# Relative attention with paired corner terms, a reordered unit, a reordered start, and reordered experts

## Chip, core and metric

The kernel runs on one core of one Trainium2 chip. The metric is the device time of one execution in microseconds (us); lower is better. All tensors are float32. Every input comes from device memory (DRAM) and the output goes back there.

## The reference, cut

Four layers follow one another on 16 sequences of 256 tokens with 128 features, each with a layer norm over the sum with its input: an attention with relative positions, six local-attention layers, a causal attention, and a mixture of experts. The change touches the first and the last.

```python
def _L0_attn_ref(x, Wq, Wk, Wv, Eq, Ek, Ev):        # 16 heads of 8
    rel = jnp.clip(r[:, None] - r[None, :], -64, 64) + 64
    q, k, v = (proj(Wq), proj(Wk), proj(Wv))
    a_q, a_k, a_v = Eq[rel], Ek[rel], Ev[rel]
    content = jnp.einsum('bhld,bhmd->bhlm', q, k)
    rel_k = jnp.einsum('bhld,lmd->bhlm', q, a_k)
    rel_q = jnp.einsum('bhmd,lmd->bhlm', k, a_q)
    pos_pos = jnp.einsum('lmd,lmd->lm', a_q, a_k)
    attn = jax.nn.softmax((content + rel_k + rel_q + pos_pos) * scale, axis=-1)
    return jnp.einsum('bhlm,bhmd->bhld', attn, v) + jnp.einsum('bhlm,lmd->bhld', attn, a_v)
```

The experts: each token takes the two best of eight experts by a softmax of gate scores (`gate_w`); an expert is `gelu(x @ w1 + b1) @ w2 + b2` with 64 hidden units.

## The kernel before

**Engines and order.** PE (TensorE) multiplies and transposes into PSUM, DVE (VectorE), ACT (ScalarE) and POOL (GpSimd) do the rest, SP sends DMAs. PSUM is given out as two tiles of 128x1024 (`big`) and four of 128x512 (`small`). Within a layer the program is a list of small steps written out by hand (`TURNS`, one row for each of eight slots; the number ahead of a step says how many batches, or units, it lags or, if negative, runs ahead). `in_order(first)` then fixes, for PE, ACT, DVE and POOL, the program's order of all instructions from index `first` on; SP is left to the scheduler. In relative attention `first` is taken after the tables' set-up.

**Relative attention.** A batch is eight units: 128 query rows (`lc`) by four heads. `weights` (a unit's logits, L501) puts into one `big` tile, for four heads, 256 key columns in two halves: `o = 0`, the 128 keys of the query's own half, and `o = 1`, the others. Two kinds of matmul add up there: transposes of stored terms (`rk3`, and `rkc3` for `o = 1`, L513) and products of 32 rows (`q` or `qe` with `ks`, L525). In the other half, relative distances beyond 64 all use one clipped row, so that only a corner of 64 keys by 64 queries (per `lc`) differs from it; `rkc3` holds a block of 128x128 for each head with that corner in it and zeros elsewhere, and the constant part sits in `qe` and `ks`. DVE (L535) adds the third term `rq3` and takes the minimum; `exponentials` (ACT, L551) and `turn_weights` (PE L570, copies by ACT or DVE) follow one and two units later, then `positions` and `values`.

The terms are made a batch ahead: `turn` and `project` (q, k; L317, L326), `rearranged` (POOL copies into the one tile `r_perm`, four stores to DRAM, L388, and four loads into `spots`, L393), `diagonal` (POOL mask, L405), `rq_half`, `rk_half` (PE L419, 32-row matmuls), `rq_corners`, `rk_corners` (PE L444, 32x64 matmuls), with copies by ACT (L458, L467) and adds by DVE (L478, L488). Slot 4 holds, in order for PE: `join`, `weights`, `rq_half`, `turn_weights`; slot 5: `rq_corners`, `weights`, `turn_weights`; slot 6: `project_v`, `weights`, `rq_half`, `positions`, `rk_half`, `rq_corners`, `turn_weights`; slot 7: `weights`, `rk_corners`, `turn_weights`.

Set-up, from L757: memsets of `rq3` and `rkc3`; loads; the tables `tq`, `tk` from `Eq`, `Ek` (`toeplitz`, L793); the product row `frow`, stored as `fx`; then windows of `evx` and `fx` loaded as `win` tiles and turned over by a matmul with `anti` (L878) into `tv`, `tvc`, `pp`, `ppc`. `run(at)` for `at` from -8 to -1 makes the terms of batch 0; the loads of x for batches 2 to 15 stand at `at == 0`.

**Experts.** Eight groups `g` of 512 tokens. `turn` and `score(h)` for four groups at a time, `choose(h)` (DVE, and one POOL step, L1812 to L1829) picks the experts; `first(g)` is the first matmul with Gelu (PE L1840, ACT L1847), `turn_gates` transposes the gates (L1854), `weigh` spreads them (PE L1865) and multiplies them onto the Gelus (DVE L1867, `e_hT`), `second` is the second matmul (L1876, L1883) with the residual (`e_y`) and moments on DVE, reciprocal root on POOL (L1897, L146), and `finish` normalises on ACT (L1907) and stores.

## Time and profile before

| | us |
|---|---|
| median of three runs (4126.4 to 4129.33) | 4128.36 |
| the profiled execution | 4126.21 |
| its span, first to last instruction | 4124.3 |
| PE busy | 4012.5 |
| DVE busy | 3285.5 |
| ACT busy | 3305.0 |
| POOL busy | 2783.4 |
| first transposes of logits (L513) | at 57.4 |
| last of them | at 716.8 |
| first instructions of the experts' loads | at 4000.5 |
| granted PE clock, mean | 0.991 |

An engine's busy time counts an instruction from its start to its end; matmuls are pipelined, so that several overlap and a busy PE need not be at its peak. "Idle <- X" is time in which an engine stood and what ended it; "issue" is a wait for nothing that the profile shows. The chain of waits is followed back from the last instruction, at each step to what released it. Lines of it read: start, length, what. Lines of the timeline read: start, length, engine, line, operation, output <- inputs, shape, how many merged.

### The profile page before, as it was taken

Reading aid. Unit: us, or ns where it says so; the run is one execution under the profiler, and the core shown is the slowest. Engines: PE = TensorE matmul, PEld = TensorE weight load, DVE = VectorE, ACT = ScalarE, POOL = GpSimd, SP = SyncE. Lnnn points to the kernel's source line nnn. Section 1 sums busy time; section 2 is a strip of 40 time slices with the busy share of each in tenths; the row PEclk is TensorE's granted clock in tenths of the full one; section 3 lists DMA queues with packets and bytes.
Section 4 is the critical chain, followed back from the end, with each engine's and each line's share of the span. In section 5 each row is a group of like instructions: output and inputs, shape, how many; then the busy total and the mean of one; then the engine's idle time right before and its main releaser. Section 6 shows DMA issues by size and latency. Waiting matters only on the chain.

```text
span 4124.3 us, 141653 instructions
## 1 busy us (share of the span) xinstructions
PE 4012.5 (97%) x57932; PEld 2937.4 (71%) x57932; DVE 3285.5 (80%) x6379; ACT 3305.0 (80%) x11434; POOL 2783.4 (67%) x3334
## 2 busy tenths in 40 slices
PE   7999999899999999999999999999999999999998
PEld 5888888567677677667767776776777767656665
DVE  4666666788888888888888888888888888779974
ACT  3777766688888888888888888888888888879973
POOL 3333332788888888888888888888888888722221
PEclk8999999999999999999999999999999999999999
DMA  2101012100000000000000000000000000000000
GB/s 62 40 29 38 31 36 64 26 16 19 21 24 19 15 20 20 25 21 20 20 25 16 19 19 20 25 21 14 21 15 24 15 16 14 9 3 2 2 8 21
DMA packets 181813, 90.03 MB, mean 22 GB/s; under 512 B 142493, under 2 KB 173220, under 8 KB 181164
## 3 DMA queue, kind: packets, MB, share of 16 engines
q1 hardware_dynamic: 181164, 80.97, 7.4%
q8 instruction: 457, 7.49, 0.8%
q14 instruction: 192, 1.57, 0.1%
HBM read 38.49 MB, written 6.31 MB: 11 GB/s over the span
## 4 chain that ended last, share of the span: by engine, by line
PE 86%; POOL 6%; ACT 3%; issue 2%; DVE 1%; DMA 1%; SPq 0%; POOLq 0%; DVEq 0%; ACTq 0%
PE small L1250 16%; PE big L1100 12%; PE small L1157 8%; PE big L1225 7%; PE big L1172 5%; PE small L1347 3%; PE small L1331 3%; PE small L1315 3%; PE small L570 3%; PE big L525 3%; POOL a_u L1139 3%; PE small L1592 3%; PE big L1548 3%; PE big L513 3%; PE small L1225 2%
## 5 line engine op out<-in xcount | busy, mean ns | idle before, releaser
L1193 ACT ACTIVATE a_pr<-a_pr,a_nb 128x64 f32<-128x64 f32 x3072 | 1024.0, 338 | 5.7 <-DVE a_nb L1186 5.7
L1121 POOL TENSOR_TENSOR a_u<-a_u,a_r 128x1024 f32<-128x1024 f32 x384 | 901.3, 2371 | 25.9 <-DVE a_r L1116 21.2
L1139 POOL TENSOR_TENSOR a_u<-a_u,a_y 128x1024 f32<-128x1024 f32 x384 | 722.9, 1904 | 15.0
L1250 PE MATMUL small<-a_vo,a_g 128*128 128x128 f32 x6144 | 718.1, 275 | 1.6 <-DVE c_st L1465 1.6
L1250 PEld LDWEIGHTS small<-a_vo,a_g 128*128 128x128 f32 x6144 | 701.6, 192 | 2.6 <-ACT a_g L1243 2.5
L1111 ACT ACTIVATE a_sq<-big 128x1024 f32<-128x1024 f32 x384 | 391.4, 1021 | 260.2 <-PE big L1100 259.5
L1193 ACT ACTIVATION_READ_ACCUMULATOR a_pr<-a_pr,a_nb 128x1 f32 x3072 | 587.9, 191 | 0.0
L1157 PEld LDWEIGHTS small<-ident,a_u 128*128 128x128 f32 x3072 | 349.7, 141 | 142.8 <-POOL a_u L1139 91.0
L1128 DVE TENSOR_REDUCE a_ss<-a_sq 128x16 f32<-128x1024 f32 x384 | 445.6, 1200 | 0.0
L1157 PE MATMUL small<-ident,a_u 128*128 128x128 f32 x3072 | 402.3, 274 | 25.3 <-POOL a_u L1139 23.4
L1100 PE MATMUL big<-w_k,a_xs 128*128 128x512 f32 x768 | 382.0, 620 | 5.1 <-DVE a_r L1116 2.1
L1205 POOL TENSOR_TENSOR a_pr<-a_pr,a_rd 128x1024 f32<-128x1024 f32 x192 | 366.1, 1907 | 13.0 <-DVE a_rd L1204 13.0
L1100 PE MATMUL big<-w_q,a_xs 128*128 128x512 f32 x768 | 361.4, 593 | 0.0
L1172 PEld LDWEIGHTS big<-a_kT,a_qT 64*32 64x32 f32 x24576 | 261.4, 105 | 124.7 <-issue 74.8
L1180 DVE TENSOR_TENSOR a_pr<-big,w_band 128x1024 f32<-128x1024 f32 x192 | 234.6, 1222 | 109.0 <-PE big L1172 109.0
L535 DVE CUSTOM_DVE_ANT_0 r_lg<-big,r_rq 128x256 f32<-128x256 f32 x512 | 186.7, 421 | 152.7 <-PE big L525 126.4
L1112 DVE TENSOR_TENSOR a_u<-big,a_tak 128x1024 f32<-128x1024 f32 x192 | 235.1, 1224 | 83.9 <-ACT a_sq L1111 83.9
L1172 PE MATMUL big<-a_kT,a_qT 64*32 64x64 f32 x24576 | 293.1, 225 | 6.4 <-POOL a_kT L1150 3.5
L1233 ACT COPY a_g<-big 128x1024 f32<-128x1024 f32 x192 | 193.7, 1009 | 107.3 <-PE small L1225 106.8
L1100 PEld LDWEIGHTS big<-w_q,a_xs 128*128 128x128 f32 x768 | 142.6, 190 | 162.6 <-issue 127.4
L551 ACT ACTIVATE r_lg<-r_lg,r_nb 128x256 f32<-128x256 f32 x512 | 254.4, 508 | 2.8 <-DVE r_nb L535 2.8
L1574 ACT ACTIVATE c_lg<-c_lg,c_nb 128x256 f32<-128x256 f32 x512 | 255.6, 513 | 0.1
(290 smaller groups left out, 9316.9 us busy)
## 6 DMA issues: line engine op xcount, KB each, us to landing
a_xm<-a_xt SPq DMA_DIRECT2D x96, 96.0 KB
r_dk<-r_rowsk SPq DMA_DIRECT2D x64, 128.0 KB
r_dq<-r_rowsq SPq DMA_DIRECT2D x64, 128.0 KB
f_xt<-xa SPq DMA_DIRECT2D x96, 64.0 KB
f_xt<-xa SPq DMA_DIRECT2D x96, 63.5 KB
a_xt<-xa SPq DMA_DIRECT2D x80, 64.0 KB
a_xt<-xa SPq DMA_DIRECT2D x80, 63.5 KB
w_k<-in_L_ffn_Wqkv_dram SPq DMA_DIRECT2D x6, 512.0 KB
```

Source lines behind the costliest of these rows:

```text
L1100: T.matmul(ps[:, c * 512 : (c + 1) * 512], lhsT=xs_of[i, b][:, t, 0:P], rhs=weights[i]["qk"[j]][:, c * 512 : (c + 1) * 512], start=True, s ...
L1111: A.activation(sq, ps3, AF.Square)
L1121: G.tensor_add(u, u, r)
L1128: V.tensor_reduce(ss[:, j], st[m]["sq", j], AX.X, ALU.add)
L1139: G.tensor_mul(u, u, bcast(y[:, j].unsqueeze(2), (P, H, DH)))
L1157: T.transpose(ps[:, k, :], u[:, o : o + P], ident)
L1172: T.matmul(ps[q0 : q0 + WIN, e, c, :], lhsT=qT[DH * e : DH * (e + 1), c, q0 : q0 + WIN], rhs=kT[DH * e : DH * (e + 1), c, t * P + q0 : t * ...
L1193: A.activation(s_["pr"][:, h], s_["pr"][:, h], AF.Exp, bias=s_["nb"][:, h : h + 1], accum_out=s_["den"][:, h : h + 1],)
L1205: G.tensor_mul(s_["pr"], s_["pr"], bcast(rd.unsqueeze(2), (P, H, DH)))
L1225: T.matmul(ps[win], lhsT=x[r, t, :], rhs=pT[r, :, o, :], start=(o == 0), stop=(o == 1),)
L1250: T.matmul(ps[:, 0:D], lhsT=st[m]["g"][:, h, :], rhs=weights[i]["vo"][:, h // 2, h % 2, :], start=(h == 0), stop=(h == H - 1),)
L1574: A.activation(lg[:, j], lg[:, j], AF.Exp, bias=nb[:, j : j + 1], scale=-1.0, accum_out=st[b, lc]["den"][:, h : h + 1],)
```

## The change

It has four parts.

1. Corner terms: `rkc3` holds two heads in one block of 128x128, the even head's corner on partitions 0 to 63 and the odd head's on 64 to 127; `rk_corners` writes each with two adds, one for each parity. One transpose, whose output is 64 columns of each of two heads, takes the place of two.
2. In `weights` the products come first, then the corner transposes, then the four of `rk3`.
3. The start: `in_order` covers SP as well and begins ahead of the set-up; batch 0's `turn`, `project` and `rearranged` (split into `there` and `back`) stand in the midst of the set-up, and the windows are loaded and turned at other places; `qe` is made in `shift`; memsets of `rq3` cover its second half alone, and some stand later.
4. Experts: `choose(h)` follows `score(h)`; `first` runs three groups ahead; `weigh(g + 1)` stands before `second(g)`; the last group's moments, normalisation (on DVE) and store are done in two halves, the first of them inside the loop of its matmuls.

```diff
-    def in_order(first):
+    def in_order(first, engines=ENGINES):
...
-            rkc3[k] = pool.tile([P, H, P], F32, name=f"r_rkc{k}")
+            rkc3[k] = pool.tile([P, H // 2, P], F32, name=f"r_rkc{k}")
...
+            if b:
+                shift(b)
+
+        def shift(b):
+            q, qe = st[b]["q"], fea.tile([P, S], F32, name="r_qe")
...
         def rearranged(b, n):
+            there(b, n)
+            back(b, n)
...
             for k in range(2):
                 rows, l0 = slice(MAXD * k, MAXD * k + MAXD), MAXD * (1 - k) + 32 * phase
-                V.tensor_add(
-                    of(rkc3, b, k)[rows, :, l0 : l0 + 32].rearrange(
-                        "p h (x g i) -> p x g h i", x=2, i=4
-                    ),
-                    ps[rows],
-                    bcast(pc[rows], (MAXD, 2, 4, H, 4)),
-                )
+                for e in range(2):
+                    V.tensor_add(
+                        of(rkc3, b, k)[MAXD * e : MAXD * e + MAXD, :, l0 : l0 + 32].rearrange(
+                            "p h (x g i) -> p x g h i", x=2, i=4
+                        ),
+                        ps[rows].rearrange("p x g (h e) i -> p e x g h i", e=2)[:, e],
+                        bcast(pc[rows], (MAXD, 2, 4, H // 2, 4)),
+                    )
...
-            for o in range(2):
-                for j, h in enumerate(hs):
-                    T.matmul(
-                        ps[:, j // 2, j % 2, o],
-                        lhsT=of(rkc3 if o else rk3, b, lc)[:, h, :],
-                        rhs=ident,
-                        is_transpose=True,
-                        start=(o == 0 and j % 2 == 0),
-                        stop=False,
-                    )
             for o in range(2):
                 for k in range(2):
...
                         lhsT=s_["qe" if o else "q"][r, L],
                         rhs=s_["ks", lc][r, x : x + 2, o, :],
-                        start=False,
-                        stop=(o == 1),
+                        start=(o == 0),
+                        stop=False,
                     )
+            for k in range(2):
+                T.matmul(
+                    ps[:, k, :, 1, MAXD * lc : MAXD * lc + MAXD],
+                    lhsT=of(rkc3, b, lc)[:, hs[2 * k] // 2, :],
...
+            for j, h in enumerate(hs):
+                T.matmul(
+                    ps[:, j // 2, j % 2, 0],
+                    lhsT=of(rk3, b, lc)[:, h, :],
...
-        G.memset(rq3[0], 0.0)
-        for k in range(2):
-            V.memset(rkc3[k], 0.0)
...
+            first = len(nc.cur_bb.bb.instructions)
             load_x(0)
+            for n in "qk":
+                nc.sync.dma_start(w[n], I[f"L0_attn_W{n}"])
...
+            turn(0)
+            project(0)
+            there(0, "k")
...
+            winv = windows("v", evx, HD, P * HD, whole)
+            back(0, "k")
+            there(0, "q")
+            nc.sync.dma_start(fx, frow)
+            winvc = windows("vc", evx, HD, MAXD * HD, corner)
+            back(0, "q")
+            for k in range(2):
+                rows, u = slice(MAXD * k, MAXD * k + MAXD), (NEXT - 1) * k
+                nc.sync.dma_start(fe[rows], fx[0:1, u : u + 1].rearrange("a b -> (a b)").partition_broadcast(MAXD))
+            winp = windows("p", fx, 1, P, whole)
+            winpc = windows("pc", fx, 1, MAXD, corner)
...
+            nc.sync.dma_start(w["v"], I["L0_attn_Wv"])
+            load_x(1)
+            nc.sync.dma_start(pick, I["pick"].rearrange("p (g m) -> p g m", g=4))
+            shift(0)
+            for k in range(2):
+                G.memset(rq3[k][:, :, 1], 0.0)
+            turned(tv.rearrange("p s d -> p (s d)"), winv, HD, P * HD, None)
+            for k in range(2):
+                V.memset(rkc3[k], 0.0)
+            for at in range(-NU, -NU + 6):
+                run(at)
+            turned(pp, winp, 1, P, None)
+            turned(ppc, winpc, 1, MAXD, fe)
+            turned(tvc.rearrange("p s d -> p (s d)"), winvc, HD, MAXD * HD, ee)
...
+        for at in range(-NU + 6, N + NU):
+            if at == -NU + 6:
+                G.memset(spread, 0.0)
+            if at == -1:
+                G.memset(rq3[2][:, :, 1], 0.0)
+                V.memset(rkc3[2], 0.0)
             if at == 0:
                 for b in range(2, NB):
                     load_x(b)
             run(at)
-        env.in_order(first)
+        env.in_order(first, (*ENGINES, mybir.EngineType.SP))
...
-        glp = ctx.enter_context(tc.tile_pool(name="e_glp", bufs=NH + 1))
+        glp = ctx.enter_context(tc.tile_pool(name="e_glp", bufs=4))
...
-            if g % 2:
+            if g in (1, 3):
                 V.tensor_copy(xT, ps)
...
+                if g == NG - 1 and k % NT == NT - 1:
+                    close(g, k // NT)
+            if g < NG - 1:
+                measure(g)
...
+        def close(g, j):
+            y = two.tile([P, NT, D], F32, name="e_yh")
+            added(y, g, j)
+            mv, rs = moments(y)
+            for t in range(NT):
+                V.tensor_scalar(
+                    y[:, t], y[:, t], mv[:, t, 0:1], rs[:, t : t + 1], ALU.subtract, ALU.mult
+                )
+            store(g, j, y)
...
             score(h)
-        choose(0)
-        for g in range(NH):
-            first(g)
+            choose(h)
+        first(0)
+        first(1)
         turn_gates(0)
         weigh(0)
-        choose(1)
+        first(2)
+        turn_gates(1)
         for g in range(NG):
-            if g + 1 < NG:
-                turn_gates(g + 1)
-            if g + NH < NG:
-                first(g + NH)
-            second(g)
+            if g + 3 < NG:
+                first(g + 3)
             if g + 1 < NG:
                 weigh(g + 1)
+            second(g)
+            if g + 2 < NG:
+                turn_gates(g + 2)
             if g:
                 finish(g - 1)
-        finish(NG - 1)
         env.in_order(begin)
```

## The prediction

> **What bounds the kernel now.** I read the page's slices first: TensorE (PE) is busy in nine tenths or more of every slice but the first and the last, and its granted clock is full except there.

> ```profile
> PE   7999999899999999999999999999999999999998
> PEclk8999999999999999999999999999999999999999
> ```

> The middle (local_layers and causal_attention, lines 900 to 1727) is not edited, so three stretches matter. First, the chain of waits of the first 58 us, before the first unit of logits (its transposes start at 57.45).

> ```profile
> 8.49 7.08 PE small L793 x16
> 31.25 5.50 DMA r_rowsq<-r_perm
> 38.30 5.43 DMA r_dq<-r_rowsq
> 43.74 2.06 DMA xb<-in_L_attn_x_dram
> 50.39 7.67 issue
> ```

> Read: batch 0's q goes through DRAM and lands only at 43.7; before that PE made the tables (L793) ahead of batch 0's projection (L326 at 18.44), and POOL's mask of q (L405) started at 45.8. It is a latency chain, PE mostly idle. Second, the timeline of PE in a steady unit.

> ```profile
> 316.12 1.09 PE L570 MATMUL small<-ident,r_lg 128*128 128x128 f32 x8
> 317.05 0.60 PE L513 MATMUL big<-ident,r_rk 128*128 128x128 f32 x4
> 317.49 0.60 PE L513 MATMUL big<-ident,r_rkc 128*128 128x128 f32 x4
> 318.02 0.70 PE L525 MATMUL big<-r_ks,r_q 32*128 32x256 f32 x4
> 318.55 0.60 PE L525 MATMUL big<-r_ks,r_qe 32*128 32x256 f32 x4
> 319.08 1.10 PE L586 MATMUL small<-r_pT,r_tv 128*32 128x64 f32 x64
> ```

> Read: starts follow each other without a wait, so PE sets the end here; four transposes take 0.44 (317.05 to 317.49), 0.109 each, though one is listed at 0.27. A batch takes 42.0 (L326 at 97.87 and, five batches on, at 308.07); ACT is busy 72% and DVE 65% between 160 and 400. Third, the chain at the end.

> ```profile
> 4104.90 0.75 DVE e_y L1886 x2
> 4107.32 1.12 DVE e_hT L1867
> 4108.48 2.36 PE small L1876 x8
> 4115.13 0.76 DVE e_y L1886 x2
> 4118.02 1.05 POOL e_rs L146
> 4119.70 0.49 ACT e_o L1907
> ```

> Read: a round of experts from group 4 on takes 10.2 and is no PE round: `second` ends, DVE adds and takes moments, only then multiplies `e_hT`, and PE stands for 2.0 to 2.6 (2.62 before 4108.48).

> **Head of attention.** Removed: the tables ahead of batch 0 and 10.5 us of POOL memsets (3 x 3.5; now three halves of `rq3`). By the issue rows (0.34 to 1.54 each), SP has sent the loads listed ahead of `there(0, "k")` by about 9.0. x goes out at 0.72; its landing is not shown: rows of other loads give 2.2 (e_gw) to 3.9 (r_extq), so 2.9 to 4.6, I take 4. Then transposes 0.7, copy 0.4, projections 2.1, two copies 0.7: k at 8 instead of 21.2. POOL's rearrangement 0.7, to 8.9. SP: four stores 2.5, to 11.5; `winv` 0.6, to 12.1; four loads 2.8 to 3.5, to 15.3; landing 5.4 after the last issue (38.30 row), and 1 to 2 more behind winv's 512 KB (a slot of the DMA row moved 291 GB/s): 22, against 36.8. POOL may rearrange q when the stores have read `r_perm` (28.35 to 29.89, 1.5): 13.8. SP: stores 2.5, `fx` 0.3, `winvc` 1.1, loads 2.8: 22.2; q's blocks land at 27.7 to 29, against 43.7.
> The new order adds waits. On SP everything now stands behind the four loads of q, so `fe`, `winp`, `winpc` (2.9) are out at 25.1 and land 3.2 after issue (26.02 to 29.20), up to 28.5 behind q. PE's `turned(pp)` waits for them; behind it in PE's order stand rq_half 1 and rk_half 1. With 1.5 for the turns and 1.6 for rq_half 1 the first rk_half runs at 31.6 instead of 47.74: **-16.1**. From there to the first logits is DVE's drain, 9.7 before and after (8.2 of L478 and L488). The x loads of batches 2 to 15 (14 x 0.6 on SP) fall between about 29 and 38, ahead of batch 1's k stores near 44, so they cost nothing; without that cover, up to 8. Bounds: -9 (each landing 3 later, twice, and one more), -18. Batch 1's k still needs its own trip (PE idles 70.2 to 72.8 already), so what four units save there, 0.9, is lost: head **-15.2**.

> **Units.** 128 units lose two of eight term transposes: 256 x 0.109 = **-27.9**. Products ahead of transposes move the changes of array shape. From rows: entering 32-row products from 128 rows costs 0.09 + 0.12 (317.82 to 318.02, then 0.53 for 4 x 0.107), leaving them 0.1 (0.53 again): 0.3 to 0.35 a pair. With rq_half directly after products (slots 4 and 6) nothing was paid; now transposes stand between: +0.35 each. Slot 7 (rk_corners after products) +0.18. Slot 5 (rq_corners before products) saves one entry and pays one shape: -0.07. Per batch 0.81, **+13.0** over 16. Bounds 0 and 17 (slot 5 saving nothing, slot 7 a whole pair).

> [...] The rows show 0.1 to 0.2 a side.

> `rk_corners` goes from two adds of 64x512 (1.39 a pair) to four of 64x256, a form with moved partitions that the trace lacks: nearest row L478 128x256, 0.35 apart, so 1.4; bounds 1.4 and 2.8 a phase. DVE's wait for PE at 311.19 (2.06) hides it; with no cover it is 1.4 x 32 = 45. Terms are needed later in the unit, which gives them 1.0 more slack. POOL, ACT and SP of a steady batch stay. Units: **-14.9**.

> **Experts.** `choose(0)` runs 6 earlier (from 4010.8, 9.0 long), but ACT's exponential of `score(1)` now waits for DVE behind it, to 4020.6; queued behind that on ACT are the table load 1.28 and the Gelus of `first(0)`, and PE waits for their PSUM. Carrying it on (Gelu from 4022.2, `first(1)` to 4026.4, gates, weigh to 4028.9, `first(2)` and `first(3)` 3.44 each, weigh 1.07, gates 0.6) `second(0)` starts at 4037.5, was 4038.5: -1.0, bounds +3 and -4. Then `e_hT` of the next group is made while `second` (4.56) runs, so rounds are PE's: 4 x 9.56 (as 4065 to 4074 shows), 2 x 6.06 (4.56 + 1.07 + 0.43), 2 x 4.56 = 59.5, was 76.5 (4038.5 to 4115.0): -17.0, and -9 if half the waits stay. Moments of the last group by halves: from PE's end DVE 1.25, POOL 1.1, DVE 0.7, store 3.0 (4121.35 to the end), 6.1 for 9.3: -3.2. Four `glp` buffers suffice: the fourth group ahead is taken after its weigh. Experts: **-21.2**.

> **Sum.** -15.2 - 14.9 - 21.2 = -51.3. The profiled execution took 4126.21, span 4124.3 and 1.9 around it; it lies 2.15 under the runs' median of 4128.36, so 4074.9 becomes **4077**.

> **The rivals.** (a) The head does not come forward: SP in strict order stops behind one landing, windows after q, and the gain is 3 (for: 13 us of the old chain are DMA trips; against: they wait on POOL and PE work that has gone): 4089. (b) Experts stay a latency chain, the Gelus late, gain 8: 4090. (c) Changes of shape are hidden under weight loads, which overlap (PEld idles only 0.17 to 0.33): 4064. (d) It does not do what it says: PE's 100% is modelled, and another engine sets the batch; units give nothing: 4092. Against: the starts above leave no room, and DVE and ACT have a third free. (e) Slower: a transposed term accumulates onto a product just written and waits for its write. Price: at most the 0.374 of a product, for each of four heads, 1.5 a unit, 191 in all: 4268. It decides from 0.40 a unit (51.3/128). Against it: L1876 adds four terms into one block at 0.11 apart.

> **How the numbers follow.** Forecast 0.46; (a) 0.14; (b) 0.14; (c) 0.13; (d) 0.05; (e) 0.06; 0.02 for no change. A change under 0.2% (8 us) can't be told from none. Faster: 0.92, same 0.02, slower 0.06. The forecast's own range is 4064 to 4090 (bounds of its terms added as independent ones); with (a) to (c) and (d) at their middle, 4055 to 4098.

> **What would show it.** First transposes of a unit at 40 to 43; a plain unit of 2.74 instead of 2.96; L326 41.1 apart; six L513-type transposes a unit; gaps of about 0.2 before L419 in slots 4 and 6; no PE idle before L1876 from group 4 on; PE's last matmul near 6 before the end. Wrong would make it: a batch at or above 42.0, DVE without idle time, or PE waiting for `winp` beyond 35.

## The result, and the profile after

The changed kernel takes **4094.12 us**, median of four runs (4091.59 to 4097.64), beside 4127.82 for the kernel before in the same series (4126.4 to 4129.33): a ratio of 0.9919, 95% interval 0.9902 to 0.9936. So it is faster by 34 us, where 51 were forecast. The profiled execution of it took 4097.64 (span 4095.9), the slowest of the four; a second profile of the same kernel, taken later beside the experiments, took 4093.36 (span 4091.6), and both are used below.

The page's slices of the changed kernel, TensorE's busy tenths and its granted clock:

```profile
PE   8999999899999999999999999999999999989999
PEclk9999999899999999999999999999999999999999
```

The first slice is fuller than before. The clock has a dent in slice 8 (717 to 819 us; 0.90 there, 0.95 in the kernel before), which begins where the attention has just handed over to the local layers. A digit 9 stands for 0.9 or more: slice 7, with 0.93, hides the stretch at half speed that is read below.

To see where the time went, I cut the span at four instructions of TensorE that both kernels have: the projections of batches 2 and 15 (L326), the first matmul of the local layers (L1100, now L1135), and the first gate scores of the experts (L1793, now L1828). Each cell is the length of a stretch in us; the forecast gives each batch of units its -0.93 (14.9 by 16).

| stretch | before | after | again | change | forecast |
|---|---|---|---|---|---|
| start to projection of batch 2 | 97.71 | 86.14 | 85.28 | -11.6, -12.4 | -16.1 |
| 13 batches, to that of batch 15 | 546.64 | 539.36 | 539.50 | -7.3, -7.1 | -12.1 |
| to the first local matmul | 87.90 | 96.36 | 93.04 | **+8.5, +5.1** | -1.9 |
| local and causal layers | 3270.60 | 3269.46 | 3269.19 | -1.1, -1.4 | 0 |
| experts | 121.45 | 104.58 | 104.59 | -16.9, -16.9 | -21.2 |
| span | 4124.3 | 4095.9 | 4091.6 | -28.4, -32.7 | -51.3 |

All three parts gained, each less than forecast, and a stretch that I had not costed gave 5 to 8 us back.

**Head.** TensorE's timeline, changed kernel (start, busy time, engine, line, operation, tiles; in brackets idle time before it and what ended it):

```profile
31.82 0.77 PE L873 MATMUL small<-r_winp,r_anti 128*128 128x128 f32 x2 [3.44 <-DMA r_winp<-r_fx]
32.38 0.53 PE L873 MATMUL small<-r_winpc,r_anti 128*128 128x64 f32 x2
32.70 2.02 PE L873 MATMUL small<-r_winvc,r_anti 128*128 128x512 f32 x2
34.65 0.58 PE L431 MATMUL big<-r_dk,r_tq 32*128 32x128 f32 x2
...
35.02 0.42 PE L431 MATMUL big<-r_dk,r_tq 32*128 32x128 f32 x2
...
35.23 0.42 PE L431 MATMUL big<-r_dk,r_tq 32*128 32x128 f32 x2
...
36.52 0.42 PE L431 MATMUL big<-r_dq,r_tk 32*128 32x128 f32 x2
```

The turned windows wait for `r_winp`, and rq_half 1 (34.65), which needs none of them, stands behind them; rk_half, the first reader of `r_dq`, begins at 36.52.

**Units.** The same view of a steady unit:

```profile
340.71 0.70 PE L530 MATMUL big<-r_ks,r_q 32*128 32x256 f32 x4
341.24 0.60 PE L530 MATMUL big<-r_ks,r_qe 32*128 32x256 f32 x4
341.77 0.44 PE L538 MATMUL big<-ident,r_rkc 128*128 128x128 f32 x2
342.04 0.60 PE L547 MATMUL big<-ident,r_rk 128*128 128x128 f32 x4
342.48 1.04 PE L593 MATMUL small<-ident,r_lg 128*128 128x128 f32 x8
343.45 0.48 PE L530 MATMUL big<-r_ks,r_q 32*128 32x256 f32 x2
```

Six transposes of terms instead of eight, and 340.71 to 343.45 is 2.74, as forecast for a plain unit. But the batch is 41.49 (539.36 by 13), not 41.1. The wait that makes most of the difference is seen at the change of batch, first on VectorE, then on TensorE:

```profile
328.87 0.08 DVE L558 DVE_READ_ACCUMULATOR2_ANT r_nb<- 128x1 f32 x1
328.87 1.73 DVE L503 TENSOR_TENSOR r_rkc<-big,r_ppc 64x256 f32<-64x256 f32 x4
```

```profile
330.65 0.69 PE L456 MATMUL big<-r_dq,r_tkc 32*64 32x64 f32 x32 [0.27 <-DVE r_rkc L503]
```

The four adds of slot 7 (1.73; two took 1.39 before) stand behind the four reductions of a unit's logits (L558), and the next corner matmuls need the PSUM that the adds still read. Before, TensorE had no such wait.

**Hand-over.** VectorE, TensorE, ScalarE and TensorE again, changed kernel:

```profile
686.66 0.29 DVE L965 TENSOR_SCALAR w_rot<-w_rot 128x256 f32<-128x256 f32 x1 [7.31 <-DMA w_qs<-in_L_ffn_q_scale_dram]
```

```profile
687.24 1.97 PE L593 MATMUL small<-ident,r_lg 128*128 128x128 f32 x8 [2.80 <-DVE r_y L664]
```

```profile
721.43 0.37 ACT L1075 COPY a_xs<-small 128x256 f32<-128x256 f32 x1 [4.83 <-DVE xb L692]
```

```profile
721.86 3.78 PE L1135 MATMUL big<-w_k,a_xs 128*128 128x512 f32 x4 [4.23 <-ACT a_xs L1075]
```

The same two places of TensorE in the kernel before:

```profile
706.73 1.09 PE L570 MATMUL small<-ident,r_lg 128*128 128x128 f32 x8 [2.06 <-DVE r_y L641]
...
732.25 1.98 PE L1100 MATMUL big<-w_k,a_xs 128*128 128x512 f32 x4 [0.58 <-ACT a_xs L1040]
```

Two stalls. A multiply of the *next* layer's rotary table (`load_rotary`) stands among VectorE's last attention instructions and waits 7.31 us for a load; TensorE stops for 2.80 and then runs eight transposes in 1.97, as against 1.04 in a steady unit: its granted clock is 0.50 there. Then ScalarE's first copy of the local layers waits for the attention's last normalise, and TensorE stops for 4.23, where it stopped 0.58 before. TensorE by stretches of 2 us (columns: length, busy time and count of PE, PEld, DVE, ACT, POOL, granted clock, DMA share, GB/s):

```profile
684.00:686.00 2.00, 0.43 (x4) 0.20 (x2) 0.00 (x0) 1.09 (x6) 0.00 (x0) 1.00 0.66 163
686.00:688.00 2.00, 0.76 (x4) 0.77 (x5) 1.34 (x7) 0.00 (x0) 0.34 (x1) 0.59 0.76 205
688.00:690.00 2.00, 2.00 (x10) 1.58 (x10) 1.91 (x9) 0.59 (x1) 0.97 (x4) 0.50 0.09 21
...
698.00:700.00 2.00, 2.00 (x56) 1.67 (x58) 1.12 (x7) 0.96 (x4) 0.00 (x0) 0.50 0.08 17
700.00:702.00 2.00, 2.00 (x62) 1.82 (x55) 0.90 (x3) 0.00 (x0) 0.00 (x0) 1.00 0.26 51
```

The clock column falls to 0.50 during the stall (0.59 is the mean of its slice) and stays there to 700: 13.6 us at half speed.

**Experts.** TensorE's timeline of two rounds and of the last one:

```profile
4070.75 1.14 PE L1900 MATMUL big<-e_wT,e_esel 32*128 32x512 f32 x8 [0.73 <-ACT e_wT L1891]
...
4077.72 1.14 PE L1900 MATMUL big<-e_wT,e_esel 32*128 32x512 f32 x8 [0.73 <-ACT e_wT L1891]
...
4086.42 1.16 PE L1912 MATMUL small<-e_w,e_hT 128*128 128x128 f32 x8 [0.66 <-DVE e_yh L1938]
```

Of the waits of 2.0 to 2.6 before `second`, nothing is left, but two of 0.73 for the copy of turned gates have appeared (a round of 6.97, where 6.06 was forecast), and one for VectorE's read of the first half.

### The profile page after: what moved, and what is told of

It is laid out like the page before. It is cut to its first block, busy times and chain, and to the rows that moved or that the text cites. A ratio compares the mean times of both kernels' runs of the same rounds, so it can differ in the third digit from the quotient of the medians.

```text
span 4095.9 us, 141197 instructions
## 1 busy us (share of the span) xinstructions
PE 4006.0 (98%) x57676; PEld 2910.4 (71%) x57676; DVE 3299.3 (81%) x6445; ACT 3298.4 (81%) x11432; POOL 2774.8 (68%) x3334
## 4 chain that ended last, share of the span: by engine, by line
PE 72%; POOL 6%; ACT 3%; issue 2%; DVE 1%; POOLq 0%; DMA 0%; DVEq 0%; ACTq 0%; SPq 0%
PE small L1285 16%; PE big L1135 13%; PE small L1192 8%; PE big L1260 7%; PE big L1207 5%; PE small L1382 3%; PE small L1366 3%; PE small L1350 3%; PE small L1627 3%; POOL a_u L1174 3%; PE big L1583 3%; PE small L1260 2%; PE small L1643 1%; ACT a_g L1268 1%; POOL a_u L1156 1%
## 5 line engine op out<-in xcount | busy, mean ns | idle before, releaser
L1192 PE MATMUL small<-ident,a_u 128*128 128x128 f32 x3072 | 403.0, 274 | 24.5 <-POOL a_u L1174 21.1
L1135 PE MATMUL big<-w_k,a_xs 128*128 128x512 f32 x768 | 382.9, 621 | 4.6 <-ACT a_xs L1075 4.2
L1135 PE MATMUL big<-w_q,a_xs 128*128 128x512 f32 x768 | 362.0, 594 | 0.6 <-DVE a_r L1151 0.6
L558 DVE CUSTOM_DVE_ANT_0 r_lg<-big,r_rq 128x256 f32<-128x256 f32 x512 | 186.7, 421 | 132.3 <-PE big L547 81.2
L1135 PEld LDWEIGHTS big<-w_q,a_xs 128*128 128x128 f32 x768 | 142.8, 191 | 163.6 <-issue 126.8
```

Of the source, the lines that this page charges most:

```text
L1135: T.matmul(ps[:, c * 512 : (c + 1) * 512], lhsT=xs_of[i, b][:, t, 0:P], rhs=weights[i]["qk"[j]][:, c * 512 : (c + 1) * 512], start=True, s ...
L1192: T.transpose(ps[:, k, :], u[:, o : o + P], ident)
```

## The experiments

Twelve runs, in four groups; within a group all kernels and the kernel before ran on the same chip. Unless said otherwise an edit is made to the changed kernel. The intervals of single edits overlap (each is some 0.15% wide on either side), so the trace of each run carries the verdict on its place, and the time only that on the whole.

### The two stalls of the hand-over

**The multiply, taken away.** The scale goes into the constant that the table is loaded from:

```diff
     rot = np.stack([cos * scale, sin * scale, cos * inv, sin * inv])
+    rot[0:2] *= f(QK_SCALE)
...
-            V.tensor_scalar_mul(rot[:, 0:2], rot[:, 0:2], QK_SCALE)
```

> The changed kernel with the rotary table's first two planes multiplied by 8 in the constant, so that VectorE's multiply of w_rot is gone. Theory of the hand-over: that multiply, put by the scheduler among VectorE's last attention instructions, waits 7.31 us for a load (w_qs), stops TensorE for 2.80 us at 687.24 and the clock falls for some 13 us after it; without it 4 to 6 us are saved (about 4089), TensorE's idle time at 687 is gone and the granted clock between 680 and 700 is full. Rival: the load's next reader waits in its place, and the time stays within 1 us of the changed kernel's 4094.

Measured: 4089.35, ratio 0.9900 (0.9886 to 0.9913). TensorE has no idle time there, and its clock in the same stretch of 20 us is full. First the changed kernel, then this run:

```profile
680.00:700.00 20.00, 17.20 (x151) 13.68 (x144) 6.98 (x35) 9.00 (x30) 1.66 (x4) 0.66 0.25 59
```

```profile
680.00:700.00 20.00, 19.20 (x280) 15.72 (x278) 11.72 (x50) 14.26 (x48) 2.16 (x6) 1.00 0.26 64
```

From the projection of batch 15 to the last product of the attention it is 67.85 us, as against 76.84 in the first profile of the changed kernel and 73.36 in the second. The load's later readers did not stop TensorE. The theory holds; the rival falls.

**The memory places, put back.** `rkc3` is half as large after the change, so every later tile lies elsewhere. The edit allocates it whole again:

```diff
-            rkc3[k] = pool.tile([P, H // 2, P], F32, name=f"r_rkc{k}")
+            rkc3[k] = pool.tile([P, H, P], F32, name=f"r_rkc{k}")[:, 0 : H // 2]
```

> The changed kernel with r_rkc allocated as large as before (16 heads, half of it unused), so that every later tile lies where it lay before. Theory of the overlay: the halved r_rkc moved a_xs and the tables onto memory that the last normalise of the attention still reads; with the old places ScalarE's wait of 4.83 us ahead of the first a_xs copy and TensorE's 4.23 us ahead of line 1135 are gone, and the time falls by 4 to 6 us (about 4089). Rival: the wait comes of the order of the instructions alone, which stays: within 1 us of 4094.

Measured: 4090.22, ratio 0.9902 (0.9888 to 0.9915). ScalarE's copy, in this run:

```profile
714.57 0.37 ACT L1075 COPY a_xs<-small 128x256 f32<-128x256 f32 x1 [1.18 <-DVE r_rd L666]
```

The wait for the last normalise is gone, and TensorE's idle time behind it is 0.58, as before. The wait of 4.2 stood in every kernel tried with the small tile, and in none with the large one (this run, the unpaired one below, and the three that add this edit to others). So the places make it. In this run's profile the way from the last product to the first local matmul is hardly shorter for it (19.06, with 19.51 and 19.68 in the changed kernel's two), because the clock stood at 0.50 from 706.0 to 712.8; where it stayed full there, in the run of both edits, it is 15.87. On which of the tiles that the normalise reads `a_xs` lies, these runs do not show.

**Both.**

> The two edits of the hand-over together: the rotary planes scaled in the constant and r_rkc allocated as large as before. Theory (two separate stalls): the gains add, 8 to 12 us below the changed kernel in the same runs, with neither the idle time at 687 nor that of 4.2 us ahead of line 1135. Rival (one shared cause, the clock that halves for some 6.5 us after any gathering of idle time): the second edit gives nothing on top of the first, 4 to 6 us in all.

> The changed kernel itself once more, beside the three variants of it that follow, as the time to compare them with; about 0.992 of the kernel before. If the half-speed stretch of the clock at 686 to 700 belongs to the kernel, it is there again; if it belongs to that one execution, it is not.

Measured: 4083.68, ratio 0.9889 (0.9874 to 0.9904); the changed kernel itself in the same series 4092.75, ratio 0.9911 (0.9895 to 0.9928). So 9.1 us between the medians, in the range of two separate stalls; neither is left in the trace.

The half-speed stretch was in the second profile of the changed kernel too, but 6.8 us long instead of 13.6. It does not belong to the kernel, though. The run of the tail's edit (below) has the changed kernel's instructions up to the experts and the same stall, and a full clock behind it:

```profile
687.45 1.09 PE L593 MATMUL small<-ident,r_lg 128*128 128x128 f32 x8 [2.18 <-DVE r_y L664]
```

```profile
680.00:700.00 20.00, 17.82 (x281) 14.73 (x273) 10.13 (x46) 10.48 (x34) 1.67 (x4) 1.00 0.25 62
```

Seven profiles have the changed start and order, and the multiply. In four the clock fell at the stall, for 13.6, 6.8, 6.8 and 3.4 us (stalls of 2.80, 2.15, 2.19 and 3.12); in three it stayed full for 19 to 20 us more (stalls of 2.35, 1.94 and 2.18). From the projection of batch 15 to the last product TensorE's same instructions took 67.85 without the stall, 70.25 with it at full clock, 73.36 with 6.8 us at half speed and 76.84 with 13.6. So the stall itself costs 2.4, and the clock's share, 0 to 6.6 here, depends on the execution.

**How much of the first stall is old?** The kernel before had it as well (2.06 us idle at 706.73). The same edit to the constant was made to the kernel before:

> The kernel before, with the rotary planes scaled in the constant and nothing of the change. Here TensorE's idle time at 706.7 was 2.06 us and the clock stayed full. If the stall belonged to the old kernel as well, 1.5 to 2.5 us are saved and no more; if the change made it, nothing is saved; if what costs is the clock that falls after such a stall, it depends on the execution whether 2 or 6 are saved.

> The kernel before, a second profile. Its first profile showed 2.06 us of idle TensorE at 706.7 and a full clock after it; without the multiply (the run above) the time fell by about 8 us, 4 to 12 by the interval, where the trace shows 2.2. If the clock falls in some executions of the old kernel too, this one may show a stretch at half speed behind that wait, 3 to 7 us longer from the last product to the first local layer; if it is full again, the rest of those 8 us lies elsewhere and stays open.

Measured: 4123.31 beside 4131.4, ratio 0.9981 (0.9972 to 0.9990). The trace shows 2.2 of it: from the projection of batch 15 to the last product 70.52, as against 72.68. The second profile of the kernel before (4124.45) has the stall again, 2.29 long, and a full clock after it, so a falling clock does not account for the other 6; where they come from stays open. So the stall is old. The half clock behind it was seen only with the change, in four profiles of seven and in none of two before; that is too few to say that the change makes it, and why the clock falls in one execution and not in another isn't settled.

### The units: order, pairs and adds

**Products first, but no pairs.** Corner terms as before: two adds, eight transposes.

```diff
-            for k in range(2):
-                T.matmul(
-                    ps[:, k, :, 1, MAXD * lc : MAXD * lc + MAXD],
-                    lhsT=of(rkc3, b, lc)[:, hs[2 * k] // 2, :],
...
+            for o in (1, 0):
+                for j, h in enumerate(hs):
+                    T.matmul(
+                        ps[:, j // 2, j % 2, o],
+                        lhsT=of(rkc3 if o else rk3, b, lc)[:, h, :],
```

> The changed kernel with the corner terms as before (one head to a block, two adds on VectorE a phase, eight transposes a unit) but the products still ahead of the transposes. The forecast's prices: 256 transposes are worth 27.9 us, and the two further adds have since shown 0.27 us of TensorE's time a batch, 4.3 us; so 23.6 us slower than the changed kernel, about 4117, period of a batch 42.84 (42.03 before and 0.81 for the changes of array shape). Rival: putting the products first costs nothing, the period is 42.03, as before, and the time about 4103.

Measured: 4115.09, ratio 0.9961 (0.9948 to 0.9975); a batch 42.95, and no wait at line 456. The rival's 4103 is 12 away. The order alone costs 0.90 a batch (42.95 less 42.05, the same thirteen batches before). The traces show where: TensorE goes from 32-row to 128-row matmuls or back 25 times a batch where it went 21 times, and the distances from start to start across these changes sum to 5.82 instead of 4.53; starts with no such change between them take 0.39 less.

**The corner adds ahead of the reductions.**

```diff
-                (0, weights),
                 (-1, rk_corners, 1),
+                (0, weights),
                 (1, normalise, 0),
```

> The changed kernel with rk_corners 1 of slot 7 ahead of the unit's logits in place of behind them. Theory: the wait of TensorE at line 456 for r_rkc (0.27 us in each batch) is the price of the four adds standing behind the four reductions; with the adds ahead of them it is gone, 4.3 us in 16 batches, about 4090. Rival: the adds then hold the reductions back, the logits' space in PSUM is freed later by as much, and the time is the same or some us longer.

Measured: 4087.96, ratio 0.9898 (0.9885 to 0.9912); a batch 41.14. VectorE in this run:

```profile
325.06 1.72 DVE L503 TENSOR_TENSOR r_rkc<-big,r_ppc 64x256 f32<-64x256 f32 x4
326.81 0.42 DVE L558 CUSTOM_DVE_ANT_0 r_lg<-big,r_rq 128x256 f32<-128x256 f32 x1
...
328.45 1.28 DVE L490 TENSOR_TENSOR r_rk<-big,r_pp 128x512 f32<-128x512 f32 x2
329.65 1.41 DVE L490 TENSOR_TENSOR r_rk<-small,r_pp 128x256 f32<-128x256 f32 x4
```

The adds come while TensorE makes the logits, the reductions follow without a gap, and between 90 and 620 us no wait of TensorE reaches 0.1 us. The wait of 0.27 was worth 0.35 a batch (41.49 less 41.14). With it gone, pairs are worth 42.95 less 41.14, 1.81 a batch.

### The head and the tail

**rq_half 1 ahead of the turned windows,** and the clearing of the third `r_rkc` on GpSimd:

```diff
+            rq_half(0, 1)
+            diagonal(0, "q")
             turned(pp, winp, 1, P, None)
             turned(ppc, winpc, 1, MAXD, fe)
+            rk_half(0, 1)
+            rq_corners(0, 1)
             turned(tvc.rearrange("p s d -> p (s d)"), winvc, HD, MAXD * HD, ee)
...
-                V.memset(rkc3[2], 0.0)
+                G.memset(rkc3[2], 0.0)
```

> The changed kernel with the turning of r_winp, r_winpc and r_winvc moved behind rq_half 1 of the first batch (the last behind rk_half 1 too), and the clearing of the third r_rkc on GpSimd instead of VectorE. Theory: the head misses its forecast (first rk_half at 31.6, measured 36.5) because TensorE waits 3.44 us for r_winp with rq_half 1 behind it in its order; with rq_half 1 ahead, the first rk_half stands at 33 to 34, the first unit's products come 2.5 to 3.5 us earlier, the time falls by as much. Rival: the mask of r_dq (its GpSimd multiply begins at 31.3 and ends at 33.2) and the half clock set the start of the units whatever the order, and less than 1 us comes out.

In its place it does what was expected. Its timeline, with the changed kernel's 36.52 for the same matmul (35.52 in the second profile):

```profile
30.78 0.46 PE L873 MATMUL small<-r_winp,r_anti 128*128 128x128 f32 x2 [1.64 <-DMA r_winp<-r_fx]
31.89 0.66 PE L873 MATMUL small<-r_winpc,r_anti 128*128 128x64 f32 x2 [0.65 <-DMA r_winpc<-r_fx]
32.49 0.58 PE L431 MATMUL big<-r_dq,r_tk 32*128 32x128 f32 x2
```

The first unit's products come at 42.27 instead of 44.97, batch 2's projection at 83.03 instead of 85.28. The second of these shows less than it seems to. In the six profiles that have the changed kernel's instructions up to there (its own two and those of the two hand-over edits, of both, and of the tail), batch 2's projection stands between 83.01 and 86.61, while the first `r_dq` matmul stands between 34.84 and 36.52, which this edit's 32.49 clearly beats. The time does not show it either: 4093.59 beside 4092.75, ratio 0.9911 (0.9896 to 0.9926), single runs from 4087.07 to 4098.65. In the profiled execution, the layers between the first transposes of `a_u` (line 1192, here 1195) and the experts took 3256.7 instead of 3252.5, and the experts 107.1 instead of 104.6. So the time is inconclusive, and the run of all edits below, which makes five at once, does not separate this one.

**The last group's halves apart:** a space in PSUM for each half, and both halves' sums ahead of the first normalise (cut):

```diff
-            po = st[g]["po"] = small()
+            last = g == NG - 1
+            po = st[g]["po"] = [small()]
+            if last:
+                po.append(small())
...
+            for j in range(2):
+                added(ys[j], g, j)
+                parts.append(moments(ys[j]))
+            for j, (mv, rs) in enumerate(parts):
```

> The changed kernel with a space in PSUM of its own for each half of the last group, and VectorE's sums and moments of the second half ahead of the first half's normalise. Theory: of the experts' shortfall, 0.85 us is TensorE's wait at 4086.4 for VectorE's read of the shared space and about 2 us VectorE's wait for GpSimd with the second half's sums queued behind it; so the distance from the last second-layer matmul to the end falls from 7.0 to about 5, TensorE's wait is gone, and the time is 2 to 3 us shorter. Rival: GpSimd's chain for the group before (e_rs, e_nm until 4088.2) sets the end in any order, and less than 0.7 us comes out.

Measured: 4091.73, ratio 0.9908 (0.9893 to 0.9923); the experts' stretch 102.83 instead of 104.59, so 1.8, just under the forecast. TensorE's wait is gone. From TensorE's last matmul to the end it is 6.1 instead of 7.0, not 5:

```profile
4084.58 0.42 DVE L1941 TENSOR_TENSOR e_yh<-small,xa 128x256 f32<-128x256 f32 x1 [0.72 <-PE small L1922]
...
4087.15 0.60 DVE L1968 TENSOR_SCALAR e_yh<-e_yh,e_mv,e_rs 128x128 f32<-128x128 f32 x2 [0.67 <-POOL e_rs L146]
```

The second half's own chain, from the end of TensorE (4084.54) to the last normalise (4087.75), is 3.2 long, and 2.9 go to the store; nothing in it waits for the group before. My 5 was too low, the 6.1 of the forecast about right, and the rival falls.

### All together

> The changed kernel with all the edits tried so far: rotary planes scaled in the constant, r_rkc allocated as large as before, rk_corners 1 ahead of the unit's logits, the turns of the head behind rq_half 1, the last group's halves apart. If each price stands by itself: 9 (hand-over, measured together), 5 (corner adds, a period of 41.14 instead of 41.5), 2.3 (head, as its trace showed at batch 2), 1.7 (tail): 18 below the changed kernel, about 4075 to 4077, a ratio to the kernel before near 0.987. If the head's and the tail's gains are lost again in the layers between (the time of the head's variant did not show them), 4079 to 4081.

> The same, and turn_gates of the group after next ahead of second instead of behind it, with three buffers for e_wT. Theory: TensorE's two waits of 0.73 us for ScalarE's copy of e_wT (rounds of 6.97 instead of 5.85 in the experts) go, 1.5 us less than the one above. Rival: ScalarE's Gelus stand ahead of that copy and the wait only moves: no difference.

Measured: 4075.0, ratio 0.9868 (0.9854 to 0.9881), and with the gates ahead of `second` 4073.71, ratio 0.9862 (0.9848 to 0.9875), the fastest of all; in that one the waits of 0.73 are gone and the two rounds took 6.13 and 5.73. The 1.3 between the two medians are less than their intervals can tell.

The first of them, cut into the same stretches as above:

| stretch | change to before | forecast of the change |
|---|---|---|
| start to projection of batch 2 | -16.2 | -16.1 |
| 13 batches | -12.4 | -12.1 |
| to the first local matmul | -4.4 | -1.9 |
| local and causal layers | +0.2 | 0 |
| experts | -21.1 | -21.2 |
| span | -53.9 | -51.3 |

With the shortfalls mended, each stretch gives about what the forecast had for it; the third gives 2.5 more, of which 2.06 is the old kernel's own stall. Two rows meet the forecast partly by chance. The first is -14.9 in the other run, with the same head. In the experts only 1.8 is the tail's edit: 2.4 come from an earlier start of `second` (32.7 after the first gate scores, where it was 35.1), at which no edit aimed. It goes with the clock: TensorE stood at 0.50 for 10.2 us of that stretch here and for 17.1 in the changed kernel, and in the head's variant, with 22.5, `second` started after 37.7. In the records of the clock it stood at 0.50 for 47 and 42 us in these two profiles, and for 78 and 75 in the changed kernel's; how much of the gain came that way is not separated.

## Why the prediction was right, and where it fell short

**The sign and the three sources were right; the forecast of 51 us was 17 too high** (4077 forecast, 4094 measured). 4094 lies outside the forecast's own range of 4064 to 4090 and inside the wider one, with the rivals, of 4055 to 4098. Of its signs, the plain unit of 2.74, the six transposes and the end of the long waits before `second` came; the batch of 41.1 (41.49) and the first transposes at 40 to 43 (47.99) did not. By its steps:

1. *Head, -15.2.* The mechanism was right: projection at 4.16 instead of 18.44, and the wait for `r_dk` is 2.57 instead of 8.36. The first unit starts at 45.98 instead of 57.45, 11.5 earlier where 16.1 were forecast. `turned(pp)` could run at 31.8, not 28.5, and behind it the 1.5 and 1.6 for the turns and rq_half 1 were taken at full clock, where the rows at 35.02 and 35.23 show matmul pairs 0.21 apart, twice the steady 0.11: first rk_half at 36.5 instead of 31.6. Then VectorE's drain, "9.7 before and after", is 11.5 (36.52 to 47.99): a clearing of `r_rkc` of 0.91 stands in it, and eight corner adds for four. The products, which need no terms, start 2.0 ahead of the first transposes; 4.9 and 1.8 less 2.0 make up the 4.6 that are missing. From there to batch 2's projection it is 40.2, as forecast, though by another way: three units run at half clock, 3.48 apart where the same instructions take 1.77 at full (340.71 to 342.48), and this takes up the wait for batch 1's `r_dk` (2.61 before). Where the clock rose earlier, as in the head's variant, that wait is there again, 2.9 to 4.0 long. In six profiles with these instructions batch 2's projection came 11.1 to 14.7 earlier than before, so part of what is missing is the execution's.
2. *Transposes, -27.9.* Right: 1.81 a batch, 29.0 in sixteen.
3. *Changes of array shape, +13.0.* Right: 0.90 a batch, 14.4, for four more changes a batch (25 for 21). Rival (c), that they are hidden, falls with the unpaired run.
4. *Corner adds hidden by VectorE's wait at 311.19.* **This step failed.** VectorE did have idle time, but in another place. The four adds took 1.73, inside the bounds of 1.4 and 2.8, and stood behind the reductions when the next corner matmuls needed their PSUM: 0.35 a batch, 5.6 in all. A wait somewhere in the batch is no cover for work at one point of it; moving the adds by one place in the list gave that cover.
5. *"The middle is not edited, so three stretches matter."* **This step failed, and by most**: 7 to 10 us. The layer that follows shares memory and instruction queues with the one that was edited. A smaller tile moved the next layer's tiles onto memory still in use (4.23 where it was 0.58), and a stall that had always been there was in both profiles of the changed kernel followed by a half clock. None of the rivals covered it. The prediction also read the nines of the clock's slices as a full clock; in the trace before, TensorE already stood at 0.50 for 3.4 us at 739.6, 749.9 and 777.2, and behind each of the four waits of 2.0 to 2.6 in the experts.
6. *Experts, -21.2.* Mechanism right, 16.9 measured. The start is 0.5 earlier, not 1.0. Rounds took 62.5 instead of 59.5: the sum had TensorE's gates and `weigh` back to back, without ScalarE's copy between them (two waits of 0.73), and not VectorE's read of PSUM that TensorE is still filling (0.66). The tail is 7.0 instead of 6.1: VectorE waits in order for GpSimd with the second half's sums behind it, which the last group's variant shows (6.1 with the sums ahead).

Of the rivals, (d), that units give nothing, and (e), that a transposed term waits for the product's write, are refuted by the steady unit (2.74 instead of 2.96, and behind the products two transposes in 0.27 and four in 0.44). (a) came true in part: `turned(pp)` waits for a landing, but the price is 4 to 5 us and not 12. Of (b) only a shortfall of 4 us is seen, not its mechanism: from group 4 on the rounds are TensorE's.

## What to carry to other kernels

Where an edit changes the size of a tile or the order of a layer's end, cost the hand-over to the next layer too: which of its tiles move onto memory still being read, and which of its instructions already stand in this layer's queues behind a load. A cost is hidden only by idle time at the place where it falls, between the last instruction that it stands behind and the first that waits for it: the four adds, without it at their place, cost 0.35 a batch. A layout that saves work in the inner loop can come with an order that costs half of it again (14.4 of 29.0 here), and both could be priced from start-to-start distances before anything was built. One profile is not enough to price a place where the clock may fall: the same instructions took 70.3, 73.4 and 76.8 us in three executions.
